# Image 0's run-up reordered: Toeplitz of images 0-3 beside products of 4-7, Toeplitz of 4-7 beside image 0's front, matrices copied to a contiguous layout

## The chip, the core and the metric

The kernel runs on one core of one Trainium2 chip. A core has five engines with queues of their own, each in order: TensorE (PE in the profile; PEld are its weight loads), VectorE (DVE), ScalarE (ACT), GpSimd (POOL) and SyncE (SP), which here only issues transfers. ACT and POOL can issue transfers too. The metric is the time of one launch on the device in microseconds, lower is better; it is the median of several runs.

## The reference, cut to what matters

Eight images of 56 x 56 tokens with 192 channels pass through four blocks, each with a group normalisation of its input and a residual: a gated Toeplitz block (L0), shifted-window attention (L1), a 3 x 3 depthwise convolution (L2) and a two-dimensional selective scan (L3). The change concerns L0:

```python
p = silu(x @ p_w.T + p_b)
q = silu(x @ q_w.T + q_b)
v = silu(x @ v_w.T + v_b)
qv = q * v                                   # 576 channels
o1 = toeplitz(qv along w, a1)                # one 56 x 56 Toeplitz matrix per channel
o2 = toeplitz(qv along h, a2)
out = (p * (o1 + o2)) @ o_w.T + o_b
```

`a1` and `a2` come from a small network of the position offset and a decay. All is float32.

## The kernel before, in words

A framework turns the Python text into one instruction stream per engine: it puts in the semaphore waits, and in the part ahead of the scans it orders the instructions of each engine by its own estimate of times. The scans at the end stand under `tc.manual_schedule()`, in the order written. On the chip every engine follows its fixed order, so an instruction that waits holds all behind it on the same engine.

The program has these stages:

1. `products(now)` for images 0 to 3. For each image: load x, group statistics (`group_stats`, with a square root on ACT), `normalize` into `xn`, then for each tile of 128 tokens six matmuls against `wqv` (lines 234 and 235; in float32 each shows as two in the profile), three Silu on ACT (line 236), and one multiplication q * v on DVE (line 237). SP stores `qv` to DRAM (line 240), six stores per four tiles.
2. `toeplitz(now)`. For each of two axes and six blocks of 96 channels, SP loads the tile `tzx` (four images in two halves each, eight loads, line 268). For each 24 channels of it SP loads the Toeplitz matrices `tm` from `ext` (two loads, line 277): a block-diagonal tile of 112 x 112 x 24, read out of a 112-row table by overlapping rows, three tiles in turn. A channel is one matmul (line 281; two passes in the profile) with `t[:, :, c]` as the weights, a column stepping by 24 elements, and `x[:, :, c]` as the moving operand of 112 columns, stepping by 96 elements. Four channels fill a PSUM tile, which DVE and ACT in turn copy back over `tzx` (line 287). POOL stores the finished tile in eight transfers (line 295). The second axis loads `tzx` in pieces of 96 elements.
3. Setup: constants; `bias` for the attention, 98 small transfers of the bias table that ACT issues (line 360); `bmask` on DVE; the convolutions' diagonal weights; zero borders of the padded images, ten stores on ACT (line 392).
4. `front(0)`: image 0's `gate` (lines 453 to 524), `attention` (to 706), `conv2` (to 793), `inner` (to 896) and `steps` (to 940), one after the other. Its compute instructions are issued through a meter that notes an estimate of each one's cost, so they all carry line 83. Beside it runs a second generator, `products(later)` and then `toeplitz(later)` for images 4 to 7: after each step of the front, the loop adds 0.55 times the step's cost to an allowance, and runs steps of the second generator (4.3 for a product tile, 1.0 for four Toeplitz channels) until it is spent. What is left of the second generator follows the front.
5. The scans of all images (lines 1059 to 1106), with the fronts of images 1 to 7 worked in between by a planner that uses the meter's costs of `front(0)`. They take most of the time and use SBUF that the Toeplitz stage gives back.

Of the kernel before, what the change touches and what calls it, by code (L numbers as in the profile page):

```python
# [15 lines left out]
F32 = mybir.dt.float32  # L16
AF = mybir.ActivationFunctionType
# [71 lines left out]
def model(ctx: ExitStack, tc: tile.TileContext, a: dict, out: bass.AP):  # L89
# [40 lines left out]
    def group_stats(x, sp, ps, mean_out, rstd_out):  # L130

        st = sp.tile([CP, 2, NCH, 6], F32, name="gn_st")
        mv = sp.tile([CP, 2, 2], F32, name="gn_mv")
        for k in range(2):
            for j in range(NCH):
                nc.vector.bn_stats(out=st[:, k, j, :], in_=x[:, k, j * CH : (j + 1) * CH])
            nc.vector.bn_aggr(out=mv[:, k, :], in_=st[:, k].rearrange("p j s -> p (j s)"))
        pm = ps.tile([128, 512], F32, name="ps_gn", tag="ps")
        nc.tensor.matmul(pm[:CP, 0:2], gmat, mv[:, :, 0], start=True, stop=True)
        nc.vector.tensor_copy(mean_out, pm[:CP, 0:2])  # L140

        dm = sp.tile([CP, 2], F32, name="gn_dm")
        nc.vector.tensor_sub(dm, mv[:, :, 0], mean_out)
        nc.vector.tensor_mul(dm, dm, dm)
        nc.vector.tensor_add(dm, dm, mv[:, :, 1])
        pv = ps.tile([128, 512], F32, name="ps_gn", tag="ps")
        nc.tensor.matmul(pv[:CP, 0:2], gmat, dm, start=True, stop=True)
        sd = sp.tile([CP, 2], F32, name="gn_sd")
        nc.scalar.activation(sd, pv[:CP, 0:2], AF.Sqrt, bias=eps5[:CP])
        nc.vector.reciprocal(rstd_out, sd)  # L150
# [54 lines left out]
    def products(images, beside):  # L205
        with (
# [8 lines left out]
            for b in images:  # L215
                x = sp.tile([CP, 2, L], F32, name="x0", bufs=1 if beside else 2)
                nc.sync.dma_start(out=x, in_=blocks(a["x"][b]))
                group_stats(x, sp, ps, stats0[:, b, :, 0], stats0[:, b, :, 1])
                xn = sp.tile([CP + 1, 2, L], F32, name="xn0")
                nc.gpsimd.memset(xn[CP : CP + 1, 1, :], 1.0)  # L220

                for k in range(2):
                    normalize(xn[:CP, k, ::-1], x[:, k], stats0[:, b, k, 0:1], stats0[:, b, k, 1:2])
                for t0 in range(0, L, 512):
# [3 lines left out]
                    for t in range(n_t):  # L228
                        tok = slice(t0 + t * p_t, t0 + (t + 1) * p_t)
                        sl = sp.tile([128, 2 * D1], F32, name="sl", bufs=3)  # L230
# [15 lines left out]
    def toeplitz(images, beside):  # L246
        G = len(images) * (H // 2)
        with (
            tc.tile_pool(name="tz", bufs=2) as sp,
            tc.tile_pool(name="tz_t", bufs=1) as tp,  # L250
            tc.tile_pool(name="tz_ps", bufs=4 if beside else 8, space=PSUM) as ps,
        ):

            tm = [tp.tile([TT, TT, TC], F32, name=f"tm{i}") for i in range(3)]
            for t in tm:
                nc.gpsimd.memset(t, 0.0)
            n_t = 0
            for ax in range(2):
                along_h = "(h u w) c -> u h w c"
                along_w = "(u h w) c -> u w h c"  # L260
                stored = "(w u h) c -> u w h c"
                size = dict(h=H, u=2) if ax == 0 else dict(w=W, u=2)
                for c0 in range(D1 // CP):
                    x = sp.tile([TT, G, CP], F32, name="tzx", bufs=2 if beside else 3)
                    for n, b in enumerate(images):
                        v = qv_d[b][c0].rearrange(along_w if ax else along_h, **size)
                        for u in range(2):
                            nc.sync.dma_start(out=x[u * W : (u + 1) * W, n * 28 : (n + 1) * 28, :], in_=v[u])
                    for c1 in range(0, CP, TC):
                        t = tm[n_t % 3]  # L270
                        n_t += 1
                        e = ext[1 - ax][(c0 * CP + c1) // TC]

                        src = bass.AP(e.tensor, e.offset, [[TC, W], [1, W * TC]])
                        for u in range(2):
                            dst = t[u * W : (u + 1) * W, u * W : (u + 1) * W, :].rearrange("p i c -> p (i c)")
                            nc.sync.dma_start(out=dst, in_=src)
                        for c2 in range(0, TC, 4):
                            po = ps.tile([TT, 4, G], F32, name="ps_tz")
                            for c in range(4):  # L280
                                nc.tensor.matmul(  # L281
                                    po[:, c, :], t[:, :, c2 + c], x[:, :, c1 + c2 + c], start=True, stop=True
                                )
                            cs = slice(c1 + c2, c1 + c2 + 4)
                            copy = nc.vector.tensor_copy if (c2 // 4) % 2 or beside else nc.scalar.copy

                            copy(  # L287
                                x[:, :, cs].rearrange("p (b g) c -> p b g c", g=28)[:, :, ::-1, :],
                                po.rearrange("p c (b g) -> p b g c", g=28),
                            )  # L290
                            yield 1.0
                    for n, b in enumerate(images):
                        v = o_d[ax][b][c0].rearrange(stored if ax else along_h, **size)
                        for u in range(2):
                            nc.gpsimd.dma_start(out=v[1 - u], in_=x[u * W : (u + 1) * W, n * 28 : (n + 1) * 28, :])  # L295
# [3 lines left out]
    for stage in (products, toeplitz):  # L299
        for _ in stage(now, False):  # L300
            pass


    with (
# [45 lines left out]


        bias, bmask, masks = carve(slab, PT_, (NH, WS, 2, WS), (4, 6, PT_), (4, PT_))
        nc.sync.dma_start(out=masks, in_=a["masks"])

        nc.gpsimd.memset(bias, 0.0)
        for i in range(WS):
            for u in range(2):
                for j in range(WS):
                    at = (i * 2 + u) * WS + j
                    nc.scalar.dma_start(  # L360
                        out=bias[at : at + 1, :, :, u, :],
                        in_=a["table"][:, WS - 1 - i : 2 * WS - 1 - i, WS - 1 - j : 2 * WS - 1 - j].unsqueeze(0),
                    )
        for m in range(4):
            nc.vector.tensor_add(
                bmask[:, m],
                bias.rearrange("p a i u j -> p a (i u j)"),
                masks[:, m : m + 1, :].to_broadcast([PT_, 6, PT_]),
            )
        nc.sync.dma_start(out=bmask_d, in_=bmask)  # L370
        ident3, cw2, cw3, dg2, dg3, edge = carve(
            slab, 128, (32,), (C // 32, 3), (DI // 32, 3), (C // 32, 3, 32), (DI // 32, 3, 32), (2, WP)
        )
        nc.sync.dma_start(out=ident3[:CP], in_=a["ident3"])
        for cw, dg, dg_d in ((cw2, dg2, dg2_d), (cw3, dg3, dg3_d)):
            n = cw.shape[1]
            nc.sync.dma_start(out=cw[:CP], in_=a["cw2" if n == C // 32 else "cw3"])
            for dx in range(3):
                nc.vector.tensor_mul(
                    dg[:CP, :, dx, :],  # L380
                    ident3[:CP].unsqueeze(1).to_broadcast([CP, n, 32]),
                    cw[:CP, :, dx : dx + 1].to_broadcast([CP, n, 32]),
                )
            nc.sync.dma_start(out=dg_d, in_=dg[:CP])

        nc.gpsimd.memset(edge, 0.0)
        for pads in (pad2_d, pad3_d):
            for pad in pads:
                n = CP if pads is pad2_d else 128
                for c in range(0, pad.shape[0], n):  # L390
                    v = pad[c : c + n].rearrange("p (h w) -> p h w", w=WP)
                    nc.scalar.dma_start(out=v[:, 0 : H + 2 : H + 1, :], in_=edge[:n])
# [807 lines left out]
        with tc.tile_pool(name="ps0", bufs=4 if later else 8, space=PSUM) as ps:  # L1200
            log = costs.setdefault("front", [])
            first, others, spent = front(0), (us for stage in (products, toeplitz) for us in stage(later, True)), 0.0
            while log_of(first, log) is not None:
                spent += 0.55 * sum(cost for _, cost in log[-1])
                while later and spent > 0.0:
                    us = next(others, None)
                    if us is None:
                        break
                    spent -= us
            for _ in others if later else ():  # L1210
                pass
# [214 lines left out]
```

## Time and profile before

| | |
|---|---|
| Time, median of 3 runs | 21470.86 us (21421.38 to 21477.67) |
| Profiled execution, its own time | 21510.71 us |
| Span of the profiled execution | 21508.5 us |
| Busy share of the span: PE, PEld, DVE, ACT, POOL | 81%, 42%, 73%, 58%, 70% |
| Mean granted TensorE clock | 0.865 |
| DMA over the span | 3470.45 MB, mean 161 GB/s |
| First and last Toeplitz matmul | 531.9 and 3373.1 us |
| First ACT exponential of the scans (line 1076) | 3418.3 us |

How to read the profile: busy time is the time in which an engine executes; a group row gives the count, total busy time, mean duration and the idle time ahead with what ended it ("<-"). Weight loads run beside matmuls, and matmuls are pipelined, so the duration of one is longer than the distance between two. The granted clock is the share of full speed that TensorE's throttle allowed. In a window row the numbers behind the engines are busy microseconds and, in brackets, the number of instructions. "SPq" and "ACTq" are transfers issued on these engines; the duration there is the time of the issue, not of the transfer.

### The profile page before, as it was taken

To read this page: it belongs to the slowest core of one execution; us is meant where nothing else is said; L and a number is where in the kernel's file an instruction comes from. 1 tells how busy PE (TensorE), PEld (TensorE's weight loads), DVE (VectorE), ACT (ScalarE), POOL (GpSimd) and SP (SyncE) were. 2 spreads that over 40 slices of the span, in tenths; PEclk is the share of its full clock that TensorE was granted. 3 is DMA by queue.
4 is the path that set the end of the run, shared out by engine and by line. 5 is a ranking of instruction groups with operands and counts; after the bars stand their busy time and mean duration, and the time that the engine had idled before them with its cause. 6 is when DMAs were issued, how large, how long until landed. Compare 5 with 4: busy or idle time off the path is not lost. (4 is left out here: it accounts for less than half of the span.)

```text
span 21508.5 us, 203992 instructions
## 1 busy us (share of the span) xinstructions
PE 17461.0 (81%) x59404; PEld 9086.2 (42%) x59404; DVE 15779.7 (73%) x12469; ACT 12490.5 (58%) x31833; POOL 15095.0 (70%) x9176
## 2 busy tenths in 40 slices
PE   7878678887887789877987788879877888787777
PEld 4845455433443344433543354334433443333333
DVE  2122116996799668977898779867987789789998
ACT  3126113666666566757575657666666667575555
POOL 0000005887788678867897778878887788689999
PEclk9587757998998889888998899889988999888888
DMA  3931676456544755466545654565446554754444
GB/s 88 248 97 39 190 211 181 131 159 213 172 142 134 217 166 152 134 183 199 160 128 172 209 157 138 159 212 170 140 148 214 173 146 132 218 180 147 134 131 128
DMA packets 2566532, 3470.45 MB, mean 161 GB/s; under 512 B 936270, under 2 KB 2518704, under 8 KB 2534578
## 3 DMA queue, kind: packets, MB, share of 16 engines
q1 hardware_dynamic: 2542724, 3340.61, 52.4%
q0 software_dynamic: 15520, 116.14, 1.5%
q8 instruction: 473, 7.75, 0.2%
q14 instruction: 647, 5.30, 0.1%
q10 hardware_dynamic: 7168, 0.65, 0.0%
HBM read 2822.68 MB, written 634.11 MB: 161 GB/s over the span
## 5 line engine op out<-in xcount | busy, mean ns | idle before, releaser
L1106 PE MATMUL ps_y<-hc,ident_sb 128*128 128x448 f32 x21504 | 10003.9, 603 | 828.4 <-POOL hc L1091 750.6
L1059 POOL TENSOR_TENSOR ring<-du,bm 128x896 f32<-128x896 f32 x5376 | 9450.8, 1775 | 745.8 <-ACT ring L1066 383.2
L1076 ACT ACTIVATE ps_a<-delta,A_logs_sb 128x449 f32<-128x449 f32 x10752 | 6859.6, 638 | 354.3 <-DVE ring L1085 97.7
L1106 PEld LDWEIGHTS ps_y<-hc,ident_sb 128*128 128x128 f32 x21504 | 4315.8, 210 | 5154.2 <-issue 3636.4
L1091 POOL TENSOR_TENSOR hc<-ring,cm 128x896 f32<-128x896 f32 x2688 | 4769.2, 1774 | 1930.7 <-DVE ring L1085 922.1
L1085 DVE TENSOR_TENSOR_SCAN ps_a<-ps_a,ring 128x898 f32<-128x898 f32 x2688 | 5428.3, 2019 | 607.8 <-ACT ps_a L1076 558.2
L1085 DVE TENSOR_TENSOR_SCAN ring<-ps_a,ring 128x898 f32<-128x898 f32 x2688 | 5424.1, 2018 | 571.8 <-ACT ps_a L1076 407.1
L1091 DVE TENSOR_TENSOR hc<-ps_a,cm 128x896 f32<-128x896 f32 x2688 | 2935.2, 1092 | 1037.6 <-PE ps_y L1106 808.0
L1098 ACT COPY state<-ps_a 128x2 f32<-128x2 f32 x2687 | 426.5, 159 | 2783.3 <-DVE hc L1091 2775.4
L287 DVE COPY tzx<-ps_tz 112x448 f32<-112x448 f32 x432 | 269.9, 625 | 1442.5 <-PE ps_tz L281 1292.4
L281 PE MATMUL ps_tz<-tzx,tm 112*112 112x112 f32 x4608 | 1031.1, 406 | 344.7 <-DMA tm<-ext 295.9
L295 POOL DMA_DIRECT2D o<-tzx x192 | 97.3, 513 | 1579.6 <-DVE tzx L287 1341.0
L281 PEld LDWEIGHTS ps_tz<-tzx,tm 112*112 112x112 f32 x4608 | 1021.8, 319 | 385.7 <-issue 381.9
L1066 ACT COPY ring<-state 128x2 f32<-128x2 f32 x4608 | 823.0, 179 | 532.2 <-POOL hc L1091 531.1
L666 PE MATMUL ps_f<-ident_sb,slab 98*98 98x98 f32 x1344 | 336.5, 325 | 602.9 <-ACT slab L659 602.7
L1098 ACT COPY state<-ring 128x2 f32<-128x2 f32 x2688 | 504.1, 188 | 489.6 <-DVE ring L1085 476.2
L1042 POOL TENSOR_TENSOR du<-delta,xcd 128x448 f32<-128x448 f32 x672 | 659.8, 982 | 20.0 <-DMA slab<-in_w_p_dram 19.6
L83 PE MATMUL ps_f<-slab 96*32 96x448 f32 (+7 forms) x2432 | 588.4, 548 | 75.9 <-DMA slab<-pad 55.9
L234 PE MATMUL ps_qv<-wqv,xn 96*128 96x384 f32 (+1 forms) x1200 | 530.3, 525 | 135.6 <-ACT sl L236 68.0
L666 PEld LDWEIGHTS ps_f<-ident_sb,slab 98*98 98x98 f32 x1344 | 202.5, 157 | 1017.5 <-ACT slab L659 798.5
L503 PE MATMUL ps_f<-ident_sb,slab 112*96 112x112 f32 x4704 | 534.7, 268 | 99.7 <-DVE slab L511 49.8
L503 PEld LDWEIGHTS ps_f<-ident_sb,slab 112*96 112x96 f32 x4704 | 513.1, 170 | 239.0 <-issue 121.6
(221 smaller groups left out, 16398.9 us busy)
## 6 DMA issues: line engine op xcount, KB each, us to landing
bm<-bc SPq DMA_DIRECT2D x1792, 448.0 KB
cm<-bc SPq DMA_DIRECT2D x1792, 448.0 KB
xcd<-xc SPq DMA_DIRECT2D x840, 224.0 KB
dl<-slab SPq DMA_DIRECT2D x224, 672.0 KB
delta<-dl SPq DMA_DIRECT2D x224, 672.0 KB
slab<-pad SPq DMA_DIRECT2D x504, 232.0 KB
tzx<-qv SPq DMA_DIRECT2D x192, 588.0 KB
o<-tzx POOLq DMA_DIRECT2D x192, 588.0 KB, 14.2
```

The source lines that it names most:

```text
L83: return f(*args, **kw)
L281: nc.tensor.matmul(po[:, c, :], t[:, :, c2 + c], x[:, :, c1 + c2 + c], start=True, stop=True)
L503: nc.tensor.matmul(p[:CP, t * TT : (t + 1) * TT], ot[:, n % 2, i, t, c % 2 * CP : c % 2 * CP + CP], ident[:TT, :TT], start=i == 0, stop=i ...
L666: nc.tensor.transpose(p[:PT_, e * PT_ : (e + 1) * PT_], S[:, 3 * g + e, :], ident[:PT_, :PT_])
L1042: nc.gpsimd.tensor_mul(du[:, 0, :], deltas[i][:, d, 1 : CH + 1], xcs.pop((i, d)))
L1059: nc.gpsimd.tensor_mul(hs[:, :, tokens(i)[0]], dus[i, d].to_broadcast([128, NG, CH]), bms[i, k])
L1066: nc.scalar.copy(in_ring(g)[:, :, tokens(i)[1]], src)
L1076: nc.scalar.activation(dA[:, n, :], deltas[i][:, d, at : at + CH + 1], AF.Exp, scale=negA[:, slot, d, c : c + 1])
L1085: nc.vector.tensor_tensor_scan(h, dA, hs, 0.0, ALU.mult, ALU.add)
L1091: (nc.gpsimd if on_pool(d, k) else nc.vector).tensor_mul(hc, h[:, :, tokens(i)[0]], cms[i, k])
L1098: nc.scalar.copy(states[i][:, d, NG * k : NG * k + NG], h[:, :, tokens(i)[2]])
L1106: nc.tensor.matmul(yps[i, d][:, :CH], ident, hcs[g][:, n, :], start=k + n == 0, stop=k + n == NP + NG - 2)
```

## The change

It reorders the stages ahead of the scans, moves the setup, and changes how the Toeplitz matrices are laid out. The scans and the fronts of images 1 to 7 are untouched.

- The setup stands inside `products(now)`: at its ninth tile POOL clears `bias` and issues the 98 table transfers; mask sums, diagonal weights and the zero borders (now issued by POOL) follow the products.
- `toeplitz(now)` runs beside `products(later)`, by a helper `beside` with the factor 0.47; `toeplitz(later)` runs beside `front(0)` with the factor 0.29.
- In `products(later)` an image is loaded and normalised in halves, with one `x0` and one `xn0` buffer and two `sl` buffers.
- In `toeplitz`, `fetch(n)` loads the matrices of 24 channels into one of two row tiles, and POOL copies them to a tile `tm` with the columns of a channel contiguous; there are two such tiles, and each is fetched one step ahead. `load(m)` loads the next `tzx` when half of the present one is worked. The moving operand is as before. The loads go through the queue given: SP beside the products, ACT beside the front. All copies out of PSUM are on DVE, and there are four PSUM tiles in both stages.

```diff
-            for b in images:
-                x = sp.tile([CP, 2, L], F32, name="x0", bufs=1 if beside else 2)
-                nc.sync.dma_start(out=x, in_=blocks(a["x"][b]))
-                group_stats(x, sp, ps, stats0[:, b, :, 0], stats0[:, b, :, 1])
-                xn = sp.tile([CP + 1, 2, L], F32, name="xn0")
+                xn = sp.tile([CP + 1, 2, L], F32, name="xn0", bufs=1 if beside else 2)
                 nc.gpsimd.memset(xn[CP : CP + 1, 1, :], 1.0)
+                K = 1 if beside else 2
+                for k0 in range(0, 2, K):
+                    x = sp.tile([CP, K, L], F32, name="x0", bufs=1 if beside else 2)
+                    nc.sync.dma_start(out=x, in_=blocks(a["x"][b])[:, k0 : k0 + K])
+                    group_stats(x, sp, ps, stats0[:, b, k0 : k0 + K, 0], stats0[:, b, k0 : k0 + K, 1])
...
+                    if beside:
+                        yield 12.0
...
-    def toeplitz(images, beside):
+    def toeplitz(images, queue):
...
-            tm = [tp.tile([TT, TT, TC], F32, name=f"tm{i}") for i in range(3)]
+            rows = [tp.tile([TT, TT, TC], F32, name=f"tr{i}") for i in range(2)]
...
+            def fetch(n):
...
+                tr = rows[n % 2]
+                src = bass.AP(e.tensor, e.offset, [[TC, W], [1, W * TC]])
+                for u in range(2):
+                    dst = tr[u * W : (u + 1) * W, u * W : (u + 1) * W, :].rearrange("p i c -> p (i c)")
+                    queue.dma_start(out=dst, in_=src)
+                tms[n] = sp.tile([TT, TC, TT], F32, name="tm")
+                nc.gpsimd.tensor_copy(tms[n].rearrange("p c i -> p i c"), tr)
...
+            def load(m):
...
+                xs[m] = sp.tile([TT, G, CP], F32, name="tzx")
+                for n, b in enumerate(images):
+                    v = qv_d[b][c0].rearrange(along_w if ax else along_h, **sizes[ax])
+                    for u in range(2):
+                        queue.dma_start(out=xs[m][u * W : (u + 1) * W, n * 28 : (n + 1) * 28, :], in_=v[u])
+            load(0)
+            fetch(0)
...
+                for c1 in range(0, CP, TC):
+                    fetch(n_t + 1)
+                    t = tms.pop(n_t)
+                    n_t += 1
+                    if c1 == 2 * TC:
+                        load(m + 1)
...
-                                    po[:, c, :], t[:, :, c2 + c], x[:, :, c1 + c2 + c], start=True, stop=True
+                                po[:, c, :], t[:, c2 + c, :], x[:, :, c1 + c2 + c], start=True, stop=True
...
-    for stage in (products, toeplitz):
-        for _ in stage(now, False):
+    with tc.tile_pool(name="setup", bufs=1) as sp:
...
+        for n, _ in enumerate(products(now, False)):
+            if n == 8:
...
+                            nc.gpsimd.dma_start(
+                                out=bias[at : at + 1, :, :, u, :],
...
+    def beside(work, other, share):
+        due = 0.0
+        for us in work:
+            due += share * us
+            while due > 0.0:
+                due -= next(other, due)
+        for _ in other:
             pass
+    first = toeplitz(now, nc.sync)
+    next(first)
+    beside(products(later, True), first, 0.47)
...
-            first, others, spent = front(0), (us for stage in (products, toeplitz) for us in stage(later, True)), 0.0
...
+            first = front(0)
+            priced = (sum(cost for _, cost in log[-1]) for _ in iter(lambda: log_of(first, log), None))
+            beside(priced, toeplitz(later, nc.scalar), 0.29)
```

## The prediction

> **What bounds the kernel now.** I read the cores view first (one core, 21508.5 us, mean granted clock 0.865), then windows cut at the borders of the stages (the borders are the first and last DMA issues and matmuls of each stage), then the timeline around the two places that looked odd, then the groups. The windows carry the case; their columns are the window, its length, busy us (count) of PE, PEld, DVE, ACT and POOL, granted clock, DMA share and GB/s:
>
> ```profile
> 0.00:503.00 503.00, 417.83 (x1276) 240.29 (x1276) 134.19 (x231) 167.54 (x329) 13.80 (x10) 0.98 0.33 80
> 503.00:1103.00 600.00, 510.71 (x2304) 507.89 (x2304) 89.97 (x144) 76.67 (x144) 51.55 (x91) 0.50 0.87 233
> 1103.00:1237.00 134.00, 0.94 (x4) 0.79 (x4) 13.57 (x30) 4.47 (x5) 10.00 (x11) 0.50 0.30 81
> 1237.00:1577.00 340.00, 337.16 (x1456) 203.25 (x1457) 96.69 (x160) 97.53 (x161) 2.91 (x2) 0.98 0.45 108
> 1577.00:2160.00 583.00, 519.64 (x2020) 295.22 (x2019) 140.96 (x288) 362.41 (x1018) 2.71 (x1) 0.79 0.18 44
> 2160.00:2256.00 96.00, 75.66 (x342) 30.00 (x340) 30.59 (x54) 25.55 (x44) 0.00 (x0) 0.84 0.71 183
> 2256.00:2726.00 470.00, 298.45 (x1345) 204.75 (x1346) 53.39 (x93) 80.17 (x102) 19.04 (x27) 0.68 0.69 202
> 2726.00:3126.00 400.00, 322.91 (x1113) 240.93 (x1113) 66.86 (x107) 91.87 (x113) 16.23 (x32) 0.58 0.69 202
> 3126.00:3418.00 292.00, 177.35 (x801) 176.13 (x800) 63.11 (x101) 1.48 (x5) 20.41 (x42) 0.50 0.82 217
> 3418.00:21508.00 18090.00, 14800.32 (x48748) 7186.97 (x48748) 15090.43 (x11263) 11582.84 (x29914) 14958.36 (x8960) 0.89 0.54 164
> ```
>
> In order: products of images 0-3; their Toeplitz stage, PE nearly full and DMA at 0.87; the setup, PE empty; then image 0's front: gate and attention beside the products of 4-7, conv2, inner and steps beside the Toeplitz stage of 4-7; its tail alone; the scans. In the compiled order the rows of the scans are the same in both kernels on every engine, so 18090 us stay and the change lives in the first 3418.
>
> The setup gap in the timeline:
>
> ```profile
> 1103.41 4.05 POOL L295 DMA_DIRECT2D o<-tzx  x8 [45.18 <-DVE tzx L287]
> 1133.92 96.88 ACTq L360 DMA_DIRECT2D slab<-in_table_dram  x97
> 1237.51 1.65 PE L234 MATMUL ps_qv<-wqv,xn 96*128 96x384 f32 x2 [58.24 <-DVE xn L153]
> ```
>
> The last stores leave, ACT issues 98 tiny table DMAs, and the square root of the group statistics is queued behind them; the first product matmul comes 134 us later.
>
> **The Toeplitz matmul.** Its price decides the sum. Groups (by form), and single stretches of the timeline at a granted clock of 1.00 (window 2400 to 2420):
>
> ```profile
> L281 PE MATMUL ps_tz<-tzx,tm 112*112 112x112 f32 x4608 | 1031.1, 406 | 344.7 <-DMA tm<-ext 295.9 <-DMA zr<-slab 30.4 <-DMA slab<-pad 15.6
> L503 PE MATMUL ps_f<-ident_sb,slab 112*96 112x112 f32 x4704 | 534.7, 268 | 99.7 <-DVE slab L511 49.8 <-DMA slab<-o 35.4 <-issue 9.5
> 2406.97 1.87 PE L281 MATMUL ps_tz<-tzx,tm 112*112 112x112 f32 x8
> 2408.49 0.39 PEld L83 LDWEIGHTS ps_f<-slab 96*128 96x128 f32 x2
> 2408.67 0.56 PE L83 MATMUL ps_f<-slab 96*128 96x448 f32 x1
> ```
>
> 1031.1 / 4608 = 224 ns each against 534.7 / 4704 = 114 ns for L503, also 112 moving columns but contiguous. Eight of them take 2406.97 to 2408.67 = 212 ns each though the clock is at 1.00, so the clock is not the cause: strides are. Two are strided, the matrix (24 elements) and tzx (96 elements); the change mends the first only. Which one limits? The last Toeplitz matmul starts at 2408.45; the next matmul, with contiguous weights loaded at 2408.49, starts only at 2408.67, some 215 ns after it. In the gate, a contiguous 112-column matmul at 1283.24 is followed by one with such weights 0.096 us later. So the load would have been ready, and the moving operand alone holds PE for 186 to 215 ns (the second matmul of a burst starts 0.19 us after the first). I take 195 ns.
>
> A rule speaks otherwise in size: the Trainium skill, "TensorE: Matmul & The Clock Gate", section "LDWEIGHTS (loading the stationary operand)", counts a load by its columns, columns / 1.2 ns = 93 ns here, and lets it run beside the matmul on its own read port. Were the matrix's stride all, a pass would fall to some 100 ns: 2304 x 0.100 = 230 us a stage instead of 2304 x 0.195 = 449. The row above (215 ns behind contiguous weights) is for the second figure.
>
> **The change part by part**, against the profiled span of 21508.5 (its own time is 21510.7, which is 40 over the median of the three runs, 21470.9).
>
> 1. Setup into the first products. The 98 table DMAs go from ACT to POOL, at the ninth product tile. Nearest row: L295, 0.51 us a DMA issue on POOL, so 50 us; L360's own 0.72 on ACT gives 71. Behind them on POOL stand ten pad stores and the row of ones of image 2, whose buffer in before was filled at 187 and used near 290. Started near 95, they are out of the way by about 200. DVE's 4 x 2.8 us of mask sums fit beside 134 busy of 503. Cost 0; if POOL were twice as slow, a few tens of us. The pad stores also go from ACT to POOL.
>
> 2. Toeplitz 0-3 beside products 4-7 (stage C). The first Toeplitz matmul stays at 532. PE: 449 + 1200 product passes x 0.33 (417.83 / 1276) = 396, sum 845. DMA: 0.87 x 600 + 0.33 x 503 = 522 + 166 = 688 at a share of 1. ACT loses 144 x 0.53 = 77 us of evictions, DVE has 288 x 0.625 + about 130 = 310. POOL gains 48 copies of 2688 elements with strided writes: no such row; the memset of the same size took 2.34 us, POOL's two-input operation 1.78 us for 896, which is 5.3 for 2688. I take 4; 48 x 4 + 48 of stores = 240 us, hidden as long as a copy stays under some 17 us (900 / 48, less 1 for stores). Each matrix now has one more link (DMA, POOL, PE), two deep. The square roots (8 instead of 4) cost two 1.28 us table loads each, beside PE. PE at 94%: C = 900, from 820 to 1020. From below: 755, DMA-bound with the 1.10 that 572 / 522 shows in before.
>
> 3. Start of the front: stores land (20 us in before), constants load (8), first weights. 38 us. So the front starts at 532 + 900 + 38 = 1470 against 1237: a loss of 233.
>
> 4. Gate and attention beside Toeplitz 4-7 (stage X). By the new order 604 Toeplitz passes lie in the gate, 1700 in the attention, the last before its final eighth. Gate: PE was full, 340 less 418 product passes x 0.324 = 205 of its own, plus 604 x 0.195 = 118, plus a start: 340. Attention: 519.64 PE less 697 product passes x 0.37 = 262, taken as 290 because a lower granted clock is likely (0.58 to 0.68 beside Toeplitz against 0.79 here), plus 1700 x 0.195 = 332, plus the idle 64 as before: 690. X = 1030 against 923, a loss of 107. DMA: about 145 MB of Toeplitz traffic (233 GB/s x 600 us gives 140) and 25 of the gate in 1030 us, 165 GB/s, hidden.
>
>  ACT now issues that stage's 96 tile loads and 96 matrix loads. On SP the later loads of before read
>
> ```profile
> L268 SPq DMA_DIRECT2D tzx<-qv x50: 307/3053/17566, 2850.1 to 3317.3; - x50
> ```
>
>  (min/median/max ns), the earlier ones 769 and the matrix loads 411 to 466 at the median: 48 x 3.05 + 48 x 0.77 + 96 x 0.44 = 226 us. Here a rule makes it less: the Trainium skill, "DMA: Bandwidth & Descriptors", section "Issuing engines are not separate DMA queues", holds that issuing elsewhere saves only the sequencer's time, usually small beside the transfer. By the rule moving them is worth nothing; by the row it is 226 us in the queue that the attention's exponentials go through. Silu leaves the attention, and with it a pair of table loads (2 x 1.28 us) per switch, over some thirty steps about 80 us. I charge ACT nothing beyond the 107, since 298 + 226 - 80 of ACT lies in 690; the bounds are -80 and +226.
>
> 5. Conv2, inner, steps alone. 96 + 470 + 400 = 966 in before with 1505 Toeplitz passes among them. 966 - 1505 x 0.224 = 629. Conv2 96; inner 330 (three times the first block's 126 less its collision with the tile loads); steps 200. Sum 625, a gain of 341. Nothing of Toeplitz is then late next.
>
> 6. The tail goes: 3126 to 3418 was 292; what remains is the start of the scans, 15. A gain of 277.
>
> Sum: -233 - 107 + 341 + 277 = 278 us less; scans start at 1470 + 1030 + 625 + 15 = 3140 instead of 3418. I round to -270: span 21238, and on the scale of the median 21470.9 - 270 = 21201. A measurement of this kernel can tell about 0.3% (64 us) from no change.
>
> **The rivals.**
>
> A, the sum above, chance 0.55, its own range -400 to -120 (21070 to 21350).
>
> B, contiguous matrices do pay in full (the rule's 100 ns): C becomes DMA-bound at 755, gate 604 x 0.095 = 57 less, attention some 110 less. -270 - 145 - 57 - 110 = -580, so 20890. For it: both operands wait in the same bursts. Against it: the 215 ns. Chance 0.17.
>
> C, ACT's queue holds the front. Place: the attention, whose chain is ACT (362 busy of 583). Price: the 226 us (by medians; single issues reached 17.6), plus each load's wait for the landing of an earlier one. It decides for slower once ACT's stalls put more than 270 us on the chain, 1.4 us for each of the 192 loads. At 370 the sum is +100: 21570. For it: L268's maximum. Against it: PE has 1700 passes to run meanwhile. Chance 0.15.
>
> D, POOL's copy is dear. From 17 us a copy it bounds stage C, from about 20 us in both stages (2 x 48 x 2.8 = 270) the gain is gone. At 15 us the double chain still costs some 150: -120, 21350. No row near says over 5.3. Chance 0.08. That Toeplitz does not run beside the products is excluded by the order (about half of the rows each); other mishaps, no gain, 0.05.
>
> **How the numbers follow.** Time 21200. Range 20900 to 21540: half of B lies below, most of C above. Faster by over 0.3%: A whole, B and half of D, 0.76; within 0.3%: rest of D and the edges of A and C, 0.08; slower 0.16.
>
> **What would show it.** Right: Toeplitz matmuls at 186 to 215 ns a pass; a stage C of about 900 us with PE over 90%; attention near 690; none of the 0.50 tail; scans of 18090. A pass near 100 ns is B; ACT idle before exponentials, ended by its own loads, is C; PE waiting for tm from POOL is D. I am wrong if the scans change by over 60 us, or if stage C runs at a clock so low that the products take 0.6 us a pass.

## The result and the profile after

The changed kernel takes 21348.97 us (median of 4 runs, 21337.26 to 21352.39) against 21474.26 us for the kernel before on the same chip: ratio 0.9946, 95% interval 0.9929 to 0.9964. That is 125 us or 0.5% faster, where 270 us were forecast. The profiled execution has a span of 21335.4 us at a mean granted clock of 0.885.

The windows of the changed kernel, cut at the same borders of stages as before (window, its length, then busy us and count of PE, PEld, DVE, ACT, POOL, granted clock, DMA share, GB/s); line numbers from here on are those of the changed kernel:

```profile
0.00:482.00 482.00, 418.06 (x1276) 240.47 (x1276) 140.81 (x241) 168.38 (x330) 83.95 (x122) 0.97 0.37 90
482.00:1493.00 1011.00, 851.56 (x3536) 673.15 (x3536) 378.11 (x500) 158.42 (x316) 293.59 (x143) 0.90 0.74 179
1493.00:1532.00 39.00, 0.00 (x0) 0.00 (x0) 0.71 (x5) 1.65 (x2) 13.29 (x10) 0.53 0.72 205
1532.00:1870.00 338.00, 319.84 (x1650) 243.36 (x1651) 91.48 (x151) 44.29 (x50) 69.61 (x36) 0.95 0.74 178
1870.00:2710.00 840.00, 571.60 (x3004) 460.59 (x3002) 215.40 (x419) 204.98 (x783) 197.65 (x108) 0.74 0.51 131
2710.00:2793.00 83.00, 42.85 (x241) 13.46 (x244) 23.16 (x43) 11.52 (x17) 0.00 (x0) 0.71 0.68 179
2793.00:3072.00 279.00, 161.61 (x718) 65.06 (x717) 4.12 (x14) 79.75 (x102) 0.00 (x0) 0.73 0.62 185
3072.00:3290.00 218.00, 128.87 (x252) 50.66 (x252) 1.59 (x1) 93.90 (x119) 9.78 (x7) 0.58 0.59 192
3290.00:21335.00 18045.00, 14783.84 (x48748) 7183.54 (x48748) 15087.43 (x11263) 11577.00 (x29908) 14948.40 (x8953) 0.89 0.54 164
```

In order: products of images 0 to 3; stage C; the start of the front; gate; attention; conv2; inner; steps with the start of the scans; the scans. The scans' first exponential comes at 3287.0 us instead of 3418.3. The forecast had 3140. Two rows hold the difference: stage C with the front's start (front at 1532 instead of 1470, +62) and the attention (840 instead of 690, +150); conv2 to the scans took 580 instead of 640 (-60).

The groups of the Toeplitz matmul, its weight load and GpSimd's copy:

```profile
L312 PE MATMUL ps_tz<-tzx,tm 112*112 112x112 f32 x4608 | 927.1, 370 | 189.2 <-POOL tm L279 181.1 <-DMA tzx<-qv 5.1 <-DVE tzx L316 3.0
L312 PEld LDWEIGHTS ps_tz<-tzx,tm 112*112 112x112 f32 x4608 | 870.5, 202 | 238.6 <-POOL tm L279 189.1 <-issue 22.4 <-DVE tzx L316 3.7
L279 POOL COPY tm<-tr 112x2688 f32<-112x2688 f32 x96 | 458.7, 4800 | 1117.2 <-DMA tr<-ext 646.7 <-PE ps_tz L312 392.0 <-issue 37.4
```

From the starts of neighbouring Toeplitz matmuls the pass is 192 ns at the median (10% to 90%: 190 to 194), against 220 before (213 to 227). The copy is 4.8 us.

In the attention, the chain of starts and stops is seen in the waits (engine, line, what it waited for: us in total, times, longest) and in one stretch of the timeline (start, us, instruction, idle time before it):

```profile
ACT slab L83 <- PE ps_f L83: 325.1, 113, 15.8
PE ps_f L83 <- ACT slab L83: 189.0, 34, 23.6
ACT slab L83 <- issue: 84.3, 17, 14.9
PE ps_tz L312 <- POOL tm L279: 60.3, 9, 15.7
```

```profile
2188.76 1.72 ACT L83 ACTIVATE slab<-slab,mxs 98x98 f32<-98x98 f32 x6 [0.26 <-DVE mxs L83]
...
2190.17 14.79 ACTq L296 DMA_DIRECT2D tzx<-qv  x1
...
2190.86 0.54 PE L83 MATMUL ps_f<-slab 98*32 98x98 f32 x4
2205.00 0.40 ACT L83 COPY slab<-ps_f 98x294 f32<-98x294 f32 x1 [14.24 <-issue]
...
2205.46 0.86 PE L83 MATMUL ps_f<-slab 98*32 98x98 f32 x8 [14.05 <-ACT slab L83]
```

One tile load occupies ACT's queue for 14.79 us. ACT's next copy out of PSUM starts 14.24 us late, with "issue" as the reason, and PE idles 14.05 us for it. ACT issues 128 loads in this window and spends 157 us on them. Their median hides that (L296 on ACT: 312/314/15435 ns for minimum, median and maximum). All tile issues longer than 3.5 us are of the second axis, which is loaded in pieces of 96 elements.

In stage C the shape is another one. SP's queue and PE near its end:

```profile
1390.02 3.02 SPq L245 DMA_DIRECT2D qv<-qv  x4
1393.14 1.20 SPq L277 DMA_DIRECT2D tr<-ext  x2
1394.71 44.36 SPq L296 DMA_DIRECT2D tzx<-qv  x8
1439.18 21.41 SPq L277 DMA_DIRECT2D tr<-ext  x8
```

```profile
1455.26 3.00 PE L312 MATMUL ps_tz<-tzx,tm 112*112 112x112 f32 x14 [41.65 <-POOL tm L279]
```

The eight loads of the last tile hold SP for 44.36 us, the matrix loads follow them, GpSimd's copy waits for the matrix, and PE waits 41.65 us for the copy. There are five waits for tm in this window, 120.8 us in all; the first, of 41.3 us, is ahead of the first Toeplitz matmul.

### The profile page after: what moved, and what is told of

It is laid out like the page before. It is cut to its first block, busy times and chain, and to the rows that moved or that the text cites. A ratio compares the mean times of both kernels' runs of the same rounds, so it can differ in the third digit from the quotient of the medians.

```text
span 21335.4 us, 204096 instructions
## 1 busy us (share of the span) xinstructions
PE 17278.2 (81%) x59420; PEld 8930.3 (42%) x59420; DVE 15942.8 (75%) x12633; ACT 12339.9 (58%) x31627; POOL 15616.3 (73%) x9378
## 5 line engine op out<-in xcount | busy, mean ns | idle before, releaser
L279 POOL COPY tm<-tr 112x2688 f32<-112x2688 f32 x96 | 458.7, 4800 | 1117.2 <-DMA tr<-ext 646.7
L312 PE MATMUL ps_tz<-tzx,tm 112*112 112x112 f32 x4608 | 927.1, 370 | 189.2 <-POOL tm L279 181.1
L312 PEld LDWEIGHTS ps_tz<-tzx,tm 112*112 112x112 f32 x4608 | 870.5, 202 | 238.6 <-POOL tm L279 189.1
L316 DVE COPY tzx<-ps_tz 112x448 f32<-112x448 f32 x576 | 356.4, 622 | 744.6 <-PE ps_tz L312 705.2
L241 ACT ACTIVATE sl<-ps_qv 128x384 f32<-128x384 f32 x600 | 293.0, 490 | 755.7 <-PE ps_qv L240 612.1
L242 DVE TENSOR_TENSOR qv<-sl 128x576 f32<-128x576 f32 (+1 forms) x200 | 206.8, 1037 | 572.5 <-ACT sl L241 556.6
```

Of the source, the lines that this page charges most:

```text
L312: nc.tensor.matmul(po[:, c, :], t[:, c2 + c, :], x[:, :, c1 + c2 + c], start=True, stop=True)
```

## The experiments

The theories: **Q**, ACT's load issues hold the attention's exponentials; **P**, 1700 Toeplitz passes with their evictions crowd the attention, whoever loads; **M**, matrices come late behind other loads in one queue, which is what lengthens stage C. All ratios are to the kernel before.

**1. Later loads on SP.**

```diff
-            beside(priced, toeplitz(later, nc.scalar), 0.29)
+            beside(priced, toeplitz(later, nc.sync), 0.29)
```

> The changed kernel with the later Toeplitz stage's loads (tzx and tr, beside image 0's front) issued by SP instead of ACT; nothing else differs. Attention took 840 us against 690 forecast, and ACT issued 128 loads for 157 us in it. Theory Q (ACT's issues hold the exponentials): attention falls to 690 to 740 us and the time by 100 to 150 us. Theory P (PE, DVE and POOL passes of 1700 Toeplitz matmuls are too dense beside the attention, whoever issues loads): attention stays within 20 us of 840, the time within 30. Theory M (a matrix comes late when its load stands behind tile loads in the same queue): no gain in the wait of PE for tm (60 us in the attention), perhaps a loss, since the front's own SP loads queue there too.

Measured 21232.28 us, ratio 0.9874 (0.9860 to 0.9887): 0.7% or some 150 us faster than the changed kernel. Gate, attention, conv2, inner, and steps in its windows:

```profile
1519.00:1862.00 343.00, 322.83 (x1651) 246.92 (x1652) 93.32 (x152) 46.32 (x55) 69.90 (x36) 0.94 0.74 182
1862.00:2372.00 510.00, 426.10 (x2316) 325.26 (x2315) 163.28 (x336) 204.17 (x776) 115.41 (x60) 0.79 0.55 133
2372.00:2495.00 123.00, 65.15 (x369) 34.71 (x367) 30.35 (x56) 11.54 (x17) 13.57 (x10) 0.74 0.85 211
2495.00:2900.00 405.00, 268.31 (x1276) 174.20 (x1276) 51.52 (x85) 79.64 (x102) 65.53 (x28) 0.76 0.70 191
2900.00:3127.00 227.00, 128.91 (x252) 50.80 (x252) 0.53 (x1) 90.98 (x118) 14.01 (x17) 0.58 0.62 201
```

PE's wait for ACT in the attention fell from 189.0 to 80.3 us, its wait for tm from 60.3 to 1.0, and "issue" is gone from ACT's waits. But the attention's count of PE matmuls is lower too (2316 instead of 3004): with the loads on SP only 1000 Toeplitz passes run beside the attention, not 1688, and the rest beside conv2 and inner. So this run alone does not part Q from P.

**2. Only the tile loads on SP.** In this run and the third, `toeplitz` takes a second queue for the matrices.

```diff
-                    queue.dma_start(out=dst, in_=src)
+                    rowq.dma_start(out=dst, in_=src)
...
+    toeplitz(later, nc.sync, nc.scalar)
```

> The changed kernel with the later Toeplitz stage's tile loads (tzx) on SP, its matrix loads (tr) left on ACT. Q: the single long issues (9.5 to 15.4 us) are all tile loads, so the gain is nearly that of moving both, 80 to 150 us. P: within 30 us of the changed kernel. M: PE's wait for tm from POOL in the attention falls from 60 us to under 30, whatever the exponentials do.

Measured 21266.73 us, ratio 0.9893 (0.9880 to 0.9907), 115 us better than the changed kernel by the ratios. ACT's 54 matrix issues in the attention cost 18.4 us in all, 0.9 at most, so the harm is in the tile loads. The attention took 597 us with 1297 passes. PE waited there for ACT 101 us, 5.7 at most, and no longer for tm: in the later stage M came true, since matrices that stood behind tile loads in ACT's queue had come late.

**3. Matrix loads of stage C on ACT.**

```diff
-    first = toeplitz(now, nc.sync)
+    first = toeplitz(now, nc.sync, nc.scalar)
```

> The changed kernel with the first Toeplitz stage's matrix loads (tr) on ACT, its tile loads (tzx) left on SP; the later stage as it was. The front started at 1532 us against 1470 forecast. M: in stage C the 121 us that PE waits for tm from POOL falls to 40 or less, the front starts 50 to 80 us earlier and the time falls by as much. P (stage C is full of PE work, 852 us busy of 1011, and the waits would be taken up elsewhere): the front starts within 20 us of 1532. A third outcome is a loss: ACT's Silu evictions wait behind loads, which shows as PE waiting for ps_qv from ACT.

Measured 21411.12 us, ratio 0.9958 (0.9945 to 0.9971); the front starts at about 1580 us instead of 1532, later by 48. The interval of the whole time overlaps that of the changed kernel, so the loss shows in stage C only. PE's wait for tm from POOL left the list, and these took its place in stage C:

```profile
PE ps_tz L312 <- DMA tzx<-qv: 93.0, 3, 45.9
PE ps_tz L312 <- DVE tzx L316: 34.9, 3, 19.1
PE ps_gn L140 <- DVE gn_mv L138: 33.3, 3, 14.4
```

M in the form stated (take the matrices out of SP's queue and the stage shortens) failed: the first twelve matrix issues held ACT for 67 us, and PE then waited for tiles.

**4. No copy by GpSimd.**

```diff
-            rows = [tp.tile([TT, TT, TC], F32, name=f"tr{i}") for i in range(2)]
+            rows = [tp.tile([TT, TT, TC], F32, name=f"tr{i}") for i in range(4)]
...
-                tms[n] = sp.tile([TT, TC, TT], F32, name="tm")
-                nc.gpsimd.tensor_copy(tms[n].rearrange("p c i -> p i c"), tr)
+                tms[n] = tr
...
-                                po[:, c, :], t[:, c2 + c, :], x[:, :, c1 + c2 + c], start=True, stop=True
+                                po[:, c, :], t[:, :, c2 + c], x[:, :, c1 + c2 + c], start=True, stop=True
```

> The changed kernel without the copy by GpSimd: the matmul reads its weights with a stride of 24 elements straight from the row tile, of which there are four instead of two; order, queues and the moving operand stay. If the contiguous layout pays as measured (pass 192 instead of 220 ns), PE's Toeplitz work rises by 4608 x 0.028 = 129 us, 65 in each stage; taking POOL's 4.8 us link out gives back up to the 121 and 60 us that PE waited for it. Balance by the forecast's view (copy hidden): 60 to 130 us slower than the changed kernel. By theory M, with the late link as the larger cost: 30 to 60 us faster, and DVE's q * v multiplication back from 1.04 to 0.76 us mean.

Measured 21482.40 us, ratio 0.9988 (0.9979 to 0.9997): 0.4% or 90 us slower than the changed kernel, inside the first estimate. The pass is 220 ns again. Stage C grew by 29 us (first to last Toeplitz matmul, 1007 against 978), not by the 65 that the longer passes add, so I estimate 36 us for the copy's link there, net. That is less than PE's waits for tm, as run 4 has waits of its own for matrices straight from DMA (71.8 us), and it holds four row tiles instead of two and two. The copy pays.

**5. No tile loads in the later stage.**

```diff
+                held = [tp.tile([TT, G, CP], F32, name=f"held{i}") for i in range(2)]
...
+                if not fill:
+                    xs[m] = held[m % 2]
+                    return
                 xs[m] = sp.tile([TT, G, CP], F32, name="tzx")
```

> The changed kernel, except that the later Toeplitz stage loads no tzx tiles: it works on two tiles that are cleared once, so images 4 to 7 get a wrong Toeplitz result. ACT keeps the matrix loads (42 us in all), and in the instruction order the stage's passes still lie before conv2, as in the changed kernel, unlike in the runs with the loads on SP, where some 700 to 1300 of 2304 slid behind the attention. So this tells the queue from the density. Q (the tile loads in ACT's queue hold the exponentials): attention near the 690 us forecast, 650 to 730, against 840. P (1700 Toeplitz passes and their evictions crowd the attention, whoever loads): attention stays over 790.

One execution: 21203.43 us. The attention in the windows, and PE's wait in it:

```profile
1889.00:2560.00 671.00, 570.06 (x3003) 458.31 (x3001) 217.12 (x433) 208.47 (x786) 198.78 (x106) 0.82 0.34 105
```

```profile
PE ps_f L83 <- ACT slab L83: 84.3, 33, 4.6
```

The work is nearly the same as in the changed kernel's attention window (PE busy 570 us against 572, 1683 Toeplitz passes against 1688), and it takes 671 us instead of 840. Theory P falls. PE's waits say what the 169 us are made of: its wait for ACT fell from 189.0 to 84.3 us (the longest from 23.6 to 4.6), its wait for tm from 60.3 to nothing. So about 105 us are Q, and about 60 us are matrices that came late behind the tile loads in the same queue. Run 5 also lacks the tiles' DMA traffic (share 0.34 instead of 0.51). But runs 1 and 2, which have it, show shares of 0.55 and 0.57 in the attention, no wait for ACT above 5.7 us and at most 1 us for tm. The place of the tile loads, ACT's queue, is the cause, not their bytes.

**6 and 9. Which stride sets the pass.** Run 6 is the changed kernel with a contiguous moving operand; run 9 is run 4, whose weights step by 24 elements, with a contiguous moving operand.

```diff
-                                po[:, c, :], t[:, c2 + c, :], x[:, :, c1 + c2 + c], start=True, stop=True
+                                po[:, c, :], t[:, c2 + c, :], t[:, c2 + c, :], start=True, stop=True
```

> The changed kernel with the Toeplitz matmul's moving operand read contiguous: 112 consecutive columns of the matrix tile instead of the column of tzx that steps by 96 elements, so the Toeplitz result is wrong; weights, counts, loads and copies stay. If the moving operand's stride sets the pass, as the forecast had it, the distance between passes falls from 192 ns to about 100 (a contiguous 112-column matmul of the gate is 96). If what is left is the weight load or the fp32 pass itself, it stays above 170.

```diff
+                                po[:, c, :], t[:, :, c2 + c], ident[:TT, :TT], start=True, stop=True
```

> The kernel without the copy by GpSimd (weights stepping by 24 elements), with a contiguous 112-column moving operand (a part of the identity, so the Toeplitz result is wrong). With both operands strided a pass is 220 ns, with contiguous weights alone 192, with a contiguous moving operand alone 98. If the slower of the two operands sets the pass, strided weights alone give 98 to 220 ns: near 220 if the weight load was the limit of the old pass and near 98 to 120 if the load is hidden beside the matmul whatever its stride. The forecast's reading (the moving operand holds PE for 186 to 215 ns) says nothing of it; my guess is 190 to 220.

The groups, first of run 6, then of run 9:

```profile
L312 PE MATMUL ps_tz<-tm 112*112 112x112 f32 x4608 | 556.1, 281 | 278.2 <-POOL tm L279 263.3 <-DVE tzx L316 14.9
L312 PEld LDWEIGHTS ps_tz<-tm 112*112 112x112 f32 x4608 | 538.3, 195 | 326.6 <-POOL tm L279 272.2 <-issue 17.8 <-DVE tzx L316 17.1
```

```profile
L311 PE MATMUL ps_tz<-ident_sb,tr 112*112 112x112 f32 x4608 | 1043.0, 406 | 112.6 <-DMA tr<-ext 96.7 <-DVE tzx L315 14.9 <-DVE gn_mv L138 1.0
L311 PEld LDWEIGHTS ps_tz<-ident_sb,tr 112*112 112x112 f32 x4608 | 1040.9, 318 | 147.6 <-issue 116.0 <-DVE tzx L315 16.5 <-DVE gn_mv L138 1.3
```

Distances between passes at the median:

| weights | moving operand | ns per pass | run |
|---|---|---|---|
| stride 24 | stride 96 | 220 | before, run 4 |
| stride 24 | contiguous | 220 | run 9 |
| contiguous | stride 96 | 192 | changed kernel |
| contiguous | contiguous | 98 | run 6 |

For these strides the slower of the two operands sets the pass; they do not add. In the kernel before the weight load was the slower one (a load of 318 ns in runs 4 and 9 against 195 to 202 with contiguous weights), with the moving operand close behind. That is why contiguous weights alone give only 28 of 122 ns. Run 9 took 21439.66 us, run 6 21103.05 us, one execution each. In run 6 stage C from first to last Toeplitz matmul fell from 978 to 876 us, while PE's busy time there fell by 180, so part of it was not gained; PE's waits for tm grew from 181 to 263 us over both stages, and whether the DMA share of 0.82 also holds the stage was not tested.

**7 and 8. Tile loads in three parts; a smaller share.** Both have the later loads on SP.

```diff
-            load(0)
             fetch(0)
+            load(0)
...
-                    if c1 == 2 * TC:
-                        load(m + 1)
+                    if c1:
+                        load(m + 1, {1: range(1), 2: range(1, 3), 3: range(3, len(images))}[c1 // TC])
...
-            beside(priced, toeplitz(later, nc.scalar), 0.29)
+            beside(priced, toeplitz(later, nc.sync), 0.29)   # run 8: 0.25
```

> The changed kernel with the later stage's loads on SP (as the first run) and, in both stages, the eight tile loads cut in three parts, issued at the second, third and fourth block of 24 channels (2, 4 and 2 loads) instead of together at the third; the first matrix is fetched ahead of the first tile. M (matrix loads wait behind tile loads in SP's queue; three gaps of 24 to 42 us in stage C and its start): the front starts 40 to 80 us earlier, and the time falls by as much below that of the first run (21232 on its chip, ratio 0.9874). Rival: the tile's buffer is freed by stores that land only then, SP waits for them, and nothing or up to 30 us is gained or lost.

> As the run before it, with the share of the later Toeplitz stage beside the front 0.25 instead of 0.29. The gate is full of PE work (323 of 343 us), the steps are not (129 of 227): passes move from the gate and the attention to the inner projection and the steps. If PE is what bounds the gate and the steps have room, 10 to 40 us are gained; if the passes that are left at the end run after the steps, 20 to 60 us are lost.

Run 7: 21246.79 us, ratio 0.9885 (0.9871 to 0.9898), no better than run 1. Stage C became longer, not shorter: the front starts at about 1560 us instead of 1519 in run 1. PE's waits in stage C:

```profile
PE ps_tz L314 <- POOL tm L279: 38.8, 5, 10.8
PE ps_tz L314 <- DMA tzx<-qv: 36.6, 1, 36.6
PE ps_gn L140 <- DVE gn_mv L138: 31.8, 5, 16.6
PE ps_tz L314 <- DMA tr<-ext: 25.7, 1, 25.7
```

The wait for tm fell from 121 to 39 us as M says, and tiles and matrices straight from DMA came late instead. Run 8: 21269.71 us, ratio 0.9893 (0.9874 to 0.9912), not distinguishable from run 7; the last Toeplitz matmul moved from 2936 to 3128 us, and the scans began at 3183 instead of 3147.

**10 and 11. A contiguous moving operand in earnest.** From run 1, small copies lay eight channels of tzx out contiguous, one step ahead: by ACT in stage C (run 10), and by GpSimd in the later stage as well (run 11).

```diff
+                ys[m, c] = sp.tile([TT, P, G], F32, name="tzy")
+                packer(ys[m, c], xs[m][:, :, c : c + P].rearrange("p g c -> p c g"))
...
+                            mv = x[:, :, c1 + c2 + c] if packer is None else ys[m, at][:, off + c, :]
+                            nc.tensor.matmul(po[:, c, :], t[:, c2 + c, :], mv, start=True, stop=True)
...
+    first = toeplitz(now, nc.sync, nc.scalar.copy)
...
+            beside(priced, toeplitz(later, nc.sync, nc.gpsimd.tensor_copy), 0.29)   # run 11
```

> The kernel of the first run (later loads on SP), with the moving operand of the first Toeplitz stage laid out contiguous by ACT: 144 copies of 8 channels (896 elements) from tzx into a small tile, one step ahead. Passes fall from 192 to 98 ns in stage C, which saves PE 2304 x 0.094 = 217 us; ACT gains 144 copies of about 1 us and is busy 158 of 1005 us there. From the run with a contiguous moving operand, where stage C fell by 102 us before transfers (DMA share 0.82) and the products held it: 60 to 100 us faster than the first run, ratio near 0.983. Rival: ACT's copies wait for tile loads and hold the Silu evictions behind them; then stage C gains under 30 us or loses.

> As the run before it, and the later stage's moving operand is laid out too, by GpSimd (144 copies more, estimated at 1.6 us each from the 4.8 us of 2688 elements, on top of 48 copies of 4.8). If PE passes bound the gate and the attention, another 30 to 80 us are gained. Rival: GpSimd's queue, where these copies stand behind stores that wait for DVE, feeds PE late; then PE waits for tzy from POOL and the time is 50 us or more above the run before it.

Run 10: 21126.81 us, ratio 0.9829 (0.9816 to 0.9843), 0.45% or 97 us better than run 1. Run 11: 21079.29 us, ratio 0.9815 (0.9801 to 0.9828), the lowest median here: 1.9% faster than the kernel before, 1.3% faster than the changed one. Stage C of run 10, and the copies in run 11:

```profile
482.00:1390.00 908.00, 673.64 (x3536) 488.25 (x3536) 371.91 (x499) 405.71 (x460) 297.19 (x144) 0.86 0.82 199
```

```profile
L307 ACT COPY tzy<-tzx 112x896 f32<-112x896 f32 x144 | 250.6, 1767 | 239.2 <-PE ps_tz L328 143.0 <-DMA tzx<-qv 63.0 <-DMA tr<-ext 33.0
L307 POOL COPY tzy<-tzx 112x896 f32<-112x896 f32 x144 | 246.7, 1730 | 534.3 <-PE ps_tz L328 327.0 <-DMA tzx<-qv 129.9 <-DMA slab<-x 51.1
```

ACT's copies are 1.77 us, not the 1 us expected, and still hidden: ACT is busy 406 of 908 us in stage C. Run 11's gain over run 10 is 0.14% by the ratios, with overlapping intervals; its scans begin 28 us earlier (3010 against 3037), so a further gain is not shown.

## Why the prediction had the direction and not the size

The direction held and the time lies in the range, but the gain was 125 us instead of 270. By its own steps:

1. **Setup, cost 0**: right, and a little better. The 98 table issues on POOL span some 70 us of the products, which end at 482 us instead of 503; the first Toeplitz matmul comes at 514 instead of the assumed 532.
2. **Stage C, 900 us**: mis-sized. The pass (195 assumed, 192 measured), PE's busy sum (845 and 852) and POOL's copy (4 assumed, 4.8 measured) were right or near. What failed is reading "PE at 94%" as the stage's length: 978 us passed between the first and the last Toeplitz matmul (514 to 1492). The step named the extra link (DMA, POOL, PE) and its depth of two, but charged nothing for it below 17 us a copy. Of PE's 120.8 us of waits for tm, 41.3 lie ahead of the first Toeplitz matmul; the other 80 lie inside the stage and are as large as the 78 us that it was too long. The copy was not slow; the matrix came late, in the longest wait behind SP's tile loads. Runs 3 and 7 removed that wait and got others for it. What would bring stage C to 900 us with these operands stays open; tile loads that do not share a queue with the `qv` stores were not tried.
3. **Start of the front, 38 us after stage C**: right, 39.
4. **Gate 340**: right, 338. **Attention 690**: the step that failed is "I charge ACT nothing beyond the 107, since 298 + 226 - 80 of ACT lies in 690". Comparing ACT's busy sum with the window treats ACT as if its work could be moved about. Its loads stand in order between an exponential and the copy that PE waits for, so the long issues lie on the chain, and matrix loads wait behind them too: 840 us instead of the 671 of run 5. The term was 169 us and not nothing: about 105 in exponentials and copies of ACT, about 60 in late matrices. The first part is rival C's mechanism, at some two fifths of the 270 us at which it would have decided for slower. That run 5's 671 lies near 690 is partly luck: PE was busy 570 us where the step had 290 + 332 = 622, and idle 101 where it had 64.
5. **Conv2, inner, steps: 625 us plus 15**: measured 580, so 60 us more gain than charged, most of it in inner (279 instead of 330). Why inner was that short was not looked into.
6. **The tail goes**: right; no Toeplitz pass is left after 2661 us.

Added up: +62 - 2 + 150 - 60 = +150 against the forecast start of 3140, and the scans did start at 3287. The scans took 18045 us instead of 18090; in runs 1 and 2, where their order is the same, 18082 each, so I read nothing into that.

Run 1 reaches the forecast's gain: its scans start at 3128 us. Not quite by the forecast's route, though, since part of the Toeplitz work then lies beside conv2 and inner.

**The rule weighed in the working.** The Trainium skill, "DMA: Bandwidth & Descriptors", section "Issuing engines are not separate DMA queues", made the move to ACT worth nothing; the row made it 226 us in ACT's queue. Neither figure was measured, but the row's side was right: the choice of the issuing engine cost about 150 us (run 1, in which some passes moved too), and here the time of the issue was not small: 14.79 us in the stretch shown. Rival B took the other rule ("TensorE: Matmul & The Clock Gate", section "LDWEIGHTS (loading the stationary operand)") to a pass of 100 ns. The runs show 98 ns only when both operands are contiguous. **Rival D** is out: the copy took 4.8 us.

## What to carry to other kernels

Before a load is given to an engine that stands on a dependent chain, look at the longest and not the median time of its issues, and count them as work in that chain rather than against the engine's busy share. Count also what stands behind them in the queue: here matrices came late as well. When a strided matmul is slow, measure the pass with each operand contiguous in turn: here the slower one set it, so mending one alone gave 28 of 122 ns. A stage at 94% of an engine with a two-deep supply chain should be given the waits of that chain, not only the busy sum.

## What was not expected of the hardware

- A strided fp32 operand stretched TensorE's pass to about twice its time: one over 112 columns is 98 ns with both contiguous, 192 with the moving operand at a stride of 96 elements, 220 with the weights at a stride of 24.
- One DMA issue held an engine for many times its usual time: 0.31 us at the median, 15.4 at most for the tile loads on ACT, 19.0 for those of run 2 on SP. What makes an issue that long was not isolated.
- GpSimd's copy slowed VectorE's two-input work beside it. The multiplication q * v, first in the changed kernel, then without the copy (minimum/median/maximum ns):

```profile
L242 DVE TENSOR_TENSOR qv<-sl x200: 736/758/10456, 70.5 to 1386.0; 128x576 f32<-128x576 f32 x96, 64x576 f32<-64x576 f32 x4
```

```profile
L242 DVE TENSOR_TENSOR qv<-sl x200: 735/758/760, 70.9 to 1406.9; 128x576 f32<-128x576 f32 x96, 64x576 f32<-64x576 f32 x4
```

  The median stays, single instructions last up to 10.5 us; the mean goes from 0.76 to 1.04 us, some 56 us over 200 instructions. In the changed kernel's trace 15 of the 200 last longer than 0.8 us, and each of the 15 overlaps a copy by GpSimd.
- A strided copy on ACT took more than twice as long for an element as a contiguous pass: 1.77 us for 896 elements (1.97 ns each) against 2.45 us for 2688 (0.91 ns each), though the second is an activation and not a copy. GpSimd took 1.73 us for the same strided copy; no contiguous one was measured there.

```profile
L980 ACT ACTIVATE slab<-slab 128x2688 f32<-128x2688 f32 x98 | 239.6, 2445 | 1.1
```
